# Half a tile of padding per expert in the steady list of pairs, the other pairs behind a branch

## The chip, the cores and the metric

The kernel runs on one core of one Trainium2 chip. The core has a matrix engine (TensorE, "PE" in the profile, with its weight loads as "PEld"), a vector engine (VectorE, "DVE"), an activation engine (ScalarE, "ACT"), GpSimd ("POOL") and SyncE ("SP"), which here issues most of the transfers. The metric is the device time of one execution in microseconds (us), lower is better. Times shown for a kernel are the median of its runs with the lowest and the highest beside it.

## The reference, cut to what matters

One transformer layer over `x` of shape (4, 2048, 256), 8192 tokens in all: an adaptive layer norm, causal attention with 16 heads of 16, a second adaptive layer norm, and a mixture of experts with one shared expert.

```
x = x + ga * attention(layernorm(x) * (1 + ca) + sa)
h = layernorm(x) * (1 + cb) + sb
x = x + gb * ffn(h)
```

In `ffn` each token is sent to 4 of 16 experts: sigmoid scores with a bias, the best 2 of 4 groups, then the best 4 experts in them. Expert e computes `silu(h @ w1[e].T) * (h @ w3[e].T)` with 192 inner columns, then `@ w2[e].T`, weighted by the token's normalised score. The shared expert does the same for every token without a weight. How many tokens an expert gets depends on the data.

## The kernel before, in words

**Blocks, phases, tiles, pairs.** Tokens are worked on in 16 blocks of 512. Two phases split the blocks: phase 0 is blocks 0 to 11 (6144 tokens), phase 1 blocks 12 to 15 (2048 tokens). Within a phase every token is written four times, once for each chosen expert, into an array `xs` sorted by expert, as a row of 272 numbers (the token, its four experts and weights, its place). Each expert's rows are cut into tiles of 256 rows (`TT`), and the last tile of an expert is padded. Two tiles, mostly of different experts, are a pair, the unit of the expert stage. Since the program is fixed and the counts are not, `Phase` (L102) provides for the worst padding, 255 rows for each of 16 experts: 56 pairs in phase 0 and 24 in phase 1, 80 in all.

**`find_tiles` (L491)** counts the tiles of each expert in a phase on VectorE, and writes a table with expert and first row of each tile. A tile past the last real one repeats the last one's place, is marked as nobody's, and its results go to rows that are never read. It is worked on in full like any other.

**Attention stage (to about 2810 us).** Per pair of heads, four kinds of work are woven by hand. Other work goes in as generators: a generator's `yield` names the point where it can stop, and `Background.pull(n)` (L76) advances it by n yields. In this stage yields also carry a price in VectorE and GpSimd time and are drawn from a budget. `send(n)` (L372) is one such generator: it loads block n after attention (L378), normalises it (`normalise`, L262, with one GpSimd instruction at L273), scales it on GpSimd (L392, four instructions), turns it on TensorE (L291), computes scores, ranks them (`route`, L297, with six GpSimd instructions at L338 and a VectorE sum at L342), counts places on TensorE (L426, `pk`), and scatters 4 x 4 groups of 128 rows to `xs` with 16 indirect transfers issued by GpSimd (L477). Blocks of phase 0 are sent in the attention stage.

**Expert stage (from about 2810 us).** The loop at L1482 goes over the 80 pairs m, three loads ahead. Per pair: SyncE reads four table entries into registers and issues two loads of weights (`wt`, 640 KB each, L1224) and two of rows (`xt`, 272 KB each, L1226). TensorE turns the rows (`turn`, L1240), makes the inner values (`gu`, L1255: 24 matmuls) in two parts, `inner_a` and `inner_b`, and the outer product (`y`, L1293 and L1304: 16 matmuls). ScalarE and VectorE do the sigmoids and products (`ha`, `hb`, L1266 to L1268). `give` (L1314) is called one pair late: VectorE works out weights and places (L1320 to L1347), ScalarE and VectorE move the products out of PSUM (`yt`, L1354, L1356), and GpSimd issues four indirect transfers that scatter them to `yd`, four rows a token (L1358). So the order on every engine is written out by hand, and an instruction that waits holds up all behind it on its engine.

**Background of the expert stage.** `other(2)`, `other(1)`, `other(2)` pull 5 yields a pair at three points: after `inner_a`, before `give`, after `inner_b`. In the 56 pairs of phase 0 the list is `late`: `send` of blocks 12 to 15 and `find_tiles` of phase 1, 62 yields a block and 9. It must be through three pairs before phase 1 begins (`late.drain`). From the second pair of phase 1 the list is `rest`, which is `back()`: for each of the 16 blocks, load (`fetch`, L1372, issued at L1375) the normalised block `hTs` and the block `base`, run the shared expert (`shared`, L1392 on: TensorE `sgu` at L1398 and `y` with `wsh`), and for the blocks of phase 0 `collect` (L1381, issued at L1386, one load of 2 MB, `yg<-yd`) and `combine` (L1438: sums of the four rows on VectorE and GpSimd, L1443 to L1449, and the store of `out`, L1450). A block of phase 0 takes 9 yields, one of phase 1 six, less one for the last. What is left of `rest` after the loop is drained there. Then the four blocks of phase 1 are collected and combined.

Of the kernel before, what the change touches and what calls it, by code (L numbers as in the profile page):

```python
# [8 lines left out]
F32 = mybir.dt.float32  # L9
# [3 lines left out]
I32 = mybir.dt.int32  # L13
AF = mybir.ActivationFunctionType
ALU = mybir.AluOpType
AX = mybir.AxisListType

P = 128
# [6 lines left out]
NB = B * NQ  # L25
E, I = 16, 192
EW = 2 * 2 * I + 2 * D
N = B * T
TT = 256
# [77 lines left out]
class Phase:  # L107


    def __init__(self, blocks):  # L110
        self.blocks = blocks
        self.tokens = len(blocks) * BT

        self.region = self.tokens + TT


        self.pairs = -(-((4 * self.tokens + E * (TT - 1)) // TT) // 2)


@with_exitstack  # L120
def adaln_attention_moe(
# [17 lines left out]
    nc = tc.nc  # L139
# [37 lines left out]
    phases = [Phase(blocks) for blocks in PHASES]  # L177
# [81 lines left out]

    between = const.tile([1, 1], F32, name="between")  # L260

    def normalise(xb, pools, xn):  # L262

        mv = pools.tile([P, 4, 2], F32, tag="mv", name="mv")
        for t in range(4):
            yield 0, 0.6, 0
            st = pools.tile([P, 6], F32, tag="bst", name="bst")
            nc.vector.bn_stats(st, xb[:, t, :])
            nc.vector.bn_aggr(mv[:, t, :], st)
        yield 0, 0.2, 1.0  # L270
        rs = pools.tile([P, 4], F32, tag="rs", name="rs")
        nc.vector.tensor_scalar_add(rs, mv[:, :, 1], EPS)
        nc.gpsimd.tensor_tensor(rs, rs, mhalf, ALU.pow)  # L273
        yield 0, 0, 0
        for t in range(4):
            if t % 2 == 0:
                yield 0, 0.9, 0
            nc.vector.tensor_scalar(
                xn[:, t, :], xb[:, t, :], mv[:, t, 0:1], rs[:, t : t + 1], ALU.subtract, ALU.mult
            )  # L280
        return xn
# [12 lines left out]
            evict(hT[:, k, :], pt, k)  # L294
        return hT

    def route(lg, tp):  # L297


        sc = tp.tile([P, 4, E], F32, tag="sc", name="sc")  # L300
        nc.scalar.activation(sc, lg, AF.Exp, scale=-1.0)
        yield 0, 0.6, 0
        nc.vector.tensor_scalar_add(sc, sc, 1.0)
        nc.vector.reciprocal(sc, sc)
        sb = tp.tile([P, 4, E], F32, tag="sb", name="sb")
        nc.vector.tensor_add(sb, sc, gbias.unsqueeze(1).to_broadcast([P, 4, E]))
        yield 0, 0.9, 0

        sg = sb.rearrange("p t (g e) -> p (t g) e", e=4)
        prs = tp.tile([P, 16, 6], F32, tag="prs", name="prs", bufs=1)  # L310
        nc.vector.tensor_add(prs[:, :, 0:3], sg[:, :, 0:3], sg[:, :, 1:4])
        nc.vector.tensor_add(prs[:, :, 3:5], sg[:, :, 0:2], sg[:, :, 2:4])
        nc.vector.tensor_add(prs[:, :, 5:6], sg[:, :, 0:1], sg[:, :, 3:4])
        gs = tp.tile([P, 4, 4], F32, tag="gs", name="gs")
        nc.vector.tensor_reduce(gs.rearrange("p t g -> p (t g)"), prs, AX.X, ALU.max)
        yield 0, 0.8, 0

        def ranks(v, k, allowed):

            full = [P, 4, k, k]  # L320
            other = v.unsqueeze(2).to_broadcast(full)
# [12 lines left out]
            for out, in0, in1, op in todo:  # L334
                for t in (slice(0, 2), slice(2, 4)) if k == E else (slice(0, 4),):
                    if k == E:
                        yield 0, 0, 1.1
                    eng.tensor_tensor(out[:, t], in0[:, t], in1[:, t], op)  # L338
            yield 0, 0, 0
            yield 0, 1.2 if k == E else 0.6, 0  # L340
            rk = tp.tile([P, 4, k], F32, tag=f"rk{k}", name=f"rk{k}")
            nc.vector.tensor_reduce(rk, gt, AX.X, ALU.add)  # L342
            return rk

        rg = yield from ranks(gs, 4, None)
        am = tp.tile([P, 4, E], BF, tag="am", name="am")
        nc.vector.tensor_scalar(
            am.rearrange("p t (g e) -> p (t g) e", e=4),
            rg.rearrange("p t g -> p (t g)").unsqueeze(2).to_broadcast([P, 16, 4]),
            2.0,  # L350
            None,
            ALU.is_lt,
        )
# [12 lines left out]
        nc.vector.tensor_mul(w, w, den.unsqueeze(2).to_broadcast([P, 4, E]))  # L366
        nc.vector.tensor_scalar_mul(w, w, 2.5)
        return re, ch, w

    modbs = [None, None]  # L370

    def send(n, xp, tp, psum, tag):  # L372

        ph = phase_of[n]
        yield 0, 0, 0
# [3 lines left out]
        if modbs[1] != n // NQ:  # L379
# [6 lines left out]
        for _ in range(3):  # L386
            yield 0, 0, 0
        h = yield from normalise(xb, tp, xb)
        for m, op in ((1, ALU.mult), (0, ALU.add)):
            for t in (slice(0, 2), slice(2, 4)):  # L390
                yield 0, 0, 1.3
                nc.gpsimd.tensor_tensor(  # L392
                    h[:, t], h[:, t], modbs[0][:, m, :].unsqueeze(1).to_broadcast([P, 2, D]), op
                )
        yield 0, 0, 0
        yield 1, 0, 0

        def evict(to, pt, k):
# [4 lines left out]
        yield 0, 0, 0  # L403
        yield 1, 0, 0
        lg = psum.tile([P, 4, E], F32, tag=tag, name="lg")
        for t in range(4):
            for k in range(2):
# [4 lines left out]
                    start=(k == 0),  # L412
                    stop=(k == 1),
                )
        re, ch, w = yield from route(lg, tp)
        yield 0, 0.2, 0
        chb = tp.tile([P, 4, E], BF, tag="chb", name="chb")
        nc.vector.tensor_copy(chb, ch)
        yield 0, 0, 0
        yield 1, 0.5, 0  # L420


# [64 lines left out]
                nc.gpsimd.memset(between, 0.0)  # L487

    tabs = ctx.enter_context(tc.tile_pool(name="tabs", bufs=1))

    def find_tiles(ph):  # L491

# [67 lines left out]
        nc.vector.tensor_scalar(real, which, last, None, ALU.is_le)  # L560
        nc.vector.scalar_tensor_tensor(tab[:, :, 2], tab[:, :, 0], 5.0, real, ALU.add, ALU.mult)
        nc.vector.tensor_scalar_add(tab[:, :, 2], tab[:, :, 2], -5.0)
        tabi = tabs.tile([P, 2, 3], I32, tag="tabi", name="tabi")
        nc.vector.tensor_copy(tabi, tab)
        tabd = dram.tile([pairs, 6], I32, name="tabd" + ph.name)
# [636 lines left out]
    def bank(name, shape=(P, 2 * TT)):  # L1202
        return banks.tile(list(shape), F32, tag="b", name=name)

    pairs = [(ph, i) for ph in phases for i in range(ph.pairs)]
    wts_, xts, xTs = {}, {}, {}
    issued = []

# [183 lines left out]
    def shared(n, hT):  # L1392
# [16 lines left out]
        ha = hp.tile([P, BT], F32, tag="sha", name="sha", bufs=1)  # L1409
        nc.scalar.activation(ha, g, AF.Sigmoid)  # L1410
        yield 0, 0, 0
        nc.vector.tensor_mul(ha, ha, g)
        nc.vector.tensor_mul(ha, ha, u)
        gu = up(2 * P)
# [2 lines left out]
        for half in range(2):  # L1417
# [2 lines left out]
            nc.scalar.activation(hb[rows, :], gu[:64, cols], AF.Sigmoid)  # L1420
            parts.append((hb[rows, :], gu[:64, cols], gu[64:, cols]))
        yield 0, 0, 0
        for to, g, u in parts:
            nc.vector.tensor_mul(to, to, g)
            nc.vector.tensor_mul(to, to, u)
        yield 0, 0, 0
        pss = outer(wsh.unsqueeze(1).to_broadcast([P, 2, EW]), ha, hb)
        yield 0, 0, 0
        y = hp.tile([P, 4, D], F32, tag="sy", name="sy", bufs=1)
        for half in range(2):  # L1430
# [39 lines left out]
    budget = Budget()  # L1470
    late, rest = Background(budget), Background(budget)
    for n in phases[1].blocks:
        late.add(send(n, lp, lp, banks, "b"))
    late.add(find_tiles(phases[1]))
    split, end = phases[0].pairs, len(pairs)

    for m in range(3):
        load(m)
    held = None
# [1 line left out]
    turn(0)  # L1481
    for m in range(end + 1):  # L1482

        def other(n):

            (late if m < split else rest).pull(n)

        if m == split + 1:
            rest.add(back())
        if m < end:  # L1490
            ha = inner_a(wts_[m], xTs[m])
            other(2)
# [12 lines left out]
        other(2)  # L1505
    rest.drain()
    for n in phases[1].blocks[:2]:
        collect(n)
    for n in phases[1].blocks:
        for _ in combine(n):  # L1510
            pass
        if n + 2 in phases[1].blocks:
            collect(n + 2)


def _rope():
# [69 lines left out]
```

## Time and profile before

| what | us |
|---|---|
| median of 3 runs | 3905.32 |
| lowest and highest of them | 3895.76, 3907.83 |
| the profiled execution's own time | 3907.39 |
| its span in the trace | 3905.7 |
| busy in the span: PE, PEld | 3298.8, 1723.2 |
| busy in the span: DVE, ACT, POOL | 2585.4, 1525.6, 1522.0 |

The span runs from the first to the last profiled instruction. A busy time is the union of the engine's instructions. A row `X <- Y` in a list of waits says that engine and line X waited for Y, with the total, how often, and the longest. The granted clock (PEclk) is the share of full speed at which TensorE was let run. `sgu`, `gu`, `yd` and the like are the program's names of tiles.

### The profile page before, as it was taken

What the parts mean: (1) busy time and instruction counts of PE and PEld (TensorE: products, weight loads), DVE (VectorE), ACT (ScalarE), POOL (GpSimd) and SP (SyncE); (2) the same over time, 40 slices, a digit from 0 to 9 for tenths busy, and PEclk for the clock granted to TensorE, in tenths of its full rate; (3) what the DMA queues carried; (4) which work ended last, traced back from release to release, by engine and by line L of the source; (5) the groups of instructions that cost most, each with busy time, mean ns of one, the idle gap of its engine ahead of it and who ended that gap; (6) DMA issues with size and microseconds to landing.
All of it is one profiled execution on the core that took longest, in us unless ns stands there. A gap on an engine that the chain in (4) does not pass through costs nothing. (4 is left out here: it accounts for less than half of the span.)

```text
span 3905.7 us, 56489 instructions
## 1 busy us (share of the span) xinstructions
PE 3298.8 (84%) x20276; PEld 1723.2 (44%) x20400; DVE 2585.4 (66%) x4650; ACT 1525.6 (39%) x2188; POOL 1522.0 (39%) x2216
## 2 busy tenths in 40 slices
PE   3677988979889889888888988899888888899994
PEld 1333433434334333333433333333477676676662
DVE  2365776767776767766676777677276576667775
ACT  0233544544455544444444544455422222222220
POOL 1321243333433353244335334210155555545554
PEclk6688988989899988988988998899999898899997
DMA  5423232331333232223323322220377666688763
GB/s 163 144 84 120 98 131 101 121 118 63 109 110 123 96 117 93 81 84 102 123 101 117 104 72 71 101 96 1 114 255 242 205 226 236 216 280 303 273 248 140
DMA packets 279212, 544.96 MB, mean 140 GB/s; under 512 B 27535, under 2 KB 151439, under 8 KB 278931
## 3 DMA queue, kind: packets, MB, share of 16 engines
q1 hardware_dynamic: 249106, 461.61, 34.8%
q0 software_dynamic: 27648, 77.63, 5.3%
q8 instruction: 161, 2.64, 0.3%
q10 hardware_dynamic: 2176, 2.10, 0.2%
q14 instruction: 121, 0.98, 0.1%
HBM read 351.42 MB, written 189.81 MB: 139 GB/s over the span
## 5 line engine op out<-in xcount | busy, mean ns | idle before, releaser
L888 DVE TENSOR_REDUCE mparts<-ps 128x2 f32<-128x1024 f32 (+3 forms) x1152 | 1180.5, 1044 | 465.1 <-PE ps L878 421.1
L1154 ACT ACTIVATE e<-st 128x1024 f32<-128x1024 f32 (+3 forms) x1280 | 1078.6, 895 | 1031.3 <-PE st L1146 954.8
L878 PE MATMUL ps<-kt,qt 64*128 64x512 f32 (+3 forms) x3328 | 616.2, 415 | 187.2 <-ACT e L1154 64.8
L1087 PE MATMUL po<-e,vg 128*32 128x512 f32 (+3 forms) x5120 | 667.8, 588 | 27.4 <-POOL e L1158 15.7
L878 PEld LDWEIGHTS ps<-kt,qt 64*128 64x128 f32 x3328 | 304.7, 204 | 778.2 <-ACT e L1154 437.9
L1158 POOL TENSOR_SCALAR_AFFINE_SELECT e<-e 128x256 f32<-128x256 f32 x512 | 204.6, 410 | 964.6 <-ACT e L1154 960.7
L1255 PE MATMUL gu<-xT,wt 128*128 128x256 f32 x1920 | 462.9, 396 | 20.4 <-issue 9.5
L1358 POOL DMA_INDIRECT yd<-yt,to x320 | 315.9, 987 | 393.0 <-ACT hb L1266 200.3
L1146 PE MATMUL st<-qt,kt 64*128 64x512 f32 (+3 forms) x2560 | 461.4, 441 | 0.0
L1255 PEld LDWEIGHTS gu<-xT,wt 128*128 128x128 f32 x1920 | 370.4, 197 | 108.6 <-issue 44.0
L1139 PE MATMUL st<-mt,pick 32*128 32x512 bf16 (+3 forms) x2560 | 302.7, 375 | 74.0 <-DVE mparts L888 46.9
L477 POOL DMA_INDIRECT xs<-row,rowx x256 | 248.4, 970 | 175.0 <-DVE row L468 120.3
L911 DVE TENSOR_REDUCE mparts<-ps 128x8 f32<-128x1024 f32 x128 | 156.7, 1224 | 202.4 <-PE ps L878 191.6
L1146 PEld LDWEIGHTS st<-qt,kt 64*128 64x128 f32 x2560 | 206.1, 199 | 139.2 <-issue 127.5
L1354 ACT ACTIVATE yt<-y,of 128x256 f32<-128x256 f32 x160 | 67.1, 470 | 400.0 <-DVE is L1334 200.6
L803 POOL TENSOR_TENSOR r<-qk,rp 128x512 f32<-128x512 f32 x120 | 154.4, 1305 | 168.4 <-DVE qk L780 164.8
L1139 PEld LDWEIGHTS <-pick 32*128 32x128 bf16 x2560 | 86.9, 92 | 297.3 <-issue 285.3
L1087 PEld LDWEIGHTS po<-e,vg 128*32 128x32 f32 x5120 | 109.2, 112 | 185.8 <-issue 126.5
L749 POOL TENSOR_TENSOR low<-whole,high 128x512 fp32r<-128x512 f32 x64 | 81.4, 1271 | 258.9 <-ACT whole L676 258.7
L1293 PE MATMUL y<-wt,ha 128*128 128x256 f32 x640 | 161.7, 391 | 21.6 <-issue 18.5
L1293 PEld LDWEIGHTS y<-wt,ha 128*128 128x128 f32 x640 | 119.3, 196 | 41.8 <-issue 24.1
L776 PE MATMUL pq<-wqkv,hT 128*128 128x512 f32 x240 | 128.3, 660 | 10.4 <-ACT whole L676 8.6
(218 smaller groups left out, 3603.2 us busy)
## 6 DMA issues: line engine op xcount, KB each, us to landing
wt<-in_w_all SPq DMA_DIRECT2D x160, 640.0 KB
kt<-kd SPq DMA_DIRECT2D x124, 512.0 KB
xt<-xs SPq DMA_DIRECT2D x160, 272.0 KB
qt<-qd SPq DMA_DIRECT2D x64, 512.0 KB
yg<-yd SPq DMA_DIRECT2D x16, 2048.0 KB
vg<-vd SPq DMA_DIRECT2D x124, 168.0 KB
xb<-in_x SPq DMA_DIRECT2D x32, 512.0 KB
qd<-high SPq DMA_DIRECT2D x128, 128.0 KB
```

What stands on the lines that cost most here:

```text
L477: s_ = nc.gpsimd.indirect_dma_start(out=ph.xs[:, :], out_offset=bass.IndirectOffsetOnAxis(ap=rowx[:, n, t, j : j + 1], axis=0), in_=row[:, ...
L878: nc.tensor.matmul(ps[:, half, to : to + width], lhsT=qt[rows, q, t * P : (t + 1) * P], rhs=kt[rows, q, key : key + width], start=start, s ...
L888: nc.vector.tensor_reduce(to, ps[:, :, :width], AX.X, ALU.max)
L911: nc.vector.tensor_reduce(mine[:, :, :, 0], ps.rearrange("p h (t k) -> p h t k", k=P), AX.X, ALU.max,)
L1087: nc.tensor.matmul(po[32 * j : 32 * j + 32, off:], lhsT=va[:, k_, j * (HD + 1) : j * (HD + 1) + 32], rhs=es[j // 2][:, j % 2, off:], start ...
L1139: nc.tensor.matmul(sts[q][:, h_, off:], lhsT=pick[rows, :], rhs=mt[rows, off:], start=True, stop=False,)
L1146: nc.tensor.matmul(sts[q][:, h_, off:], lhsT=kt[rows, q, k_ * P : (k_ + 1) * P], rhs=qt[rows, q, off:], start=False, stop=True,)
L1154: nc.scalar.activation(es[q][:, :, off:], sts[q][:, :, off:], AF.Exp, scale=SCALE)
L1158: nc.gpsimd.affine_select(out=es[q][:, :, off : off + P], in_=es[q][:, :, off : off + P], compare_op=ALU.is_ge, fill=0.0, base=0, pattern= ...
L1255: nc.tensor.matmul(ps[:, c_ * TT : (c_ + 1) * TT], lhsT=wt[:, c_, k * 2 * I + cols : k * 2 * I + cols + P], rhs=xT[:, k, c_ * TT : (c_ + 1 ...
L1293: nc.tensor.matmul(pss[half][:, t, :], lhsT=ha[:, at_ : at_ + P], rhs=wt[:, half, 4 * I : 4 * I + D], start=(t == 0), stop=False, skip_gro ...
L1358: s_ = nc.gpsimd.indirect_dma_start(out=ph.yd[:, :], out_offset=bass.IndirectOffsetOnAxis(ap=to[:, t : t + 1], axis=0), in_=yt[:, t, :], i ...
```

## The change

`Phase` gets a second number of pairs, `usual`, that provides for half a tile of padding an expert: 52 pairs in phase 0 and 20 in phase 1. The loop runs over these 72 pairs. The other 4 + 4 pairs, and a second making of all sums (shared expert, collecting, combining, for all 16 blocks), stand after the loop's end in a block that runs only if a number in memory, `beyond`, is over 0: `find_tiles` sets it to the tiles of a phase past `2 * usual`, the larger of the two phases. All engines read it into a register after the loop.

The background is spread otherwise. In the expert stage `late` is pulled 3, 2, 2 a pair and `rest` 5, 3, 4. `send` in this stage has `apart=3`: at the points where one engine's result is waited for, three empty yields in place of one (in the attention stage it stays at one). `shared` gets five more empty yields: one after each group of sigmoids, two before the outer product, and one after it. So a `send` has 76 yields in this stage, and a block of `rest` 14, or 11 in phase 1.

```diff
@@ class Phase
         self.pairs = -(-((4 * self.tokens + E * (TT - 1)) // TT) // 2)
+        self.usual = -(-(4 * self.tokens + E * TT // 2) // (2 * TT))
...
@@ normalise, route, send: empty yields
-        yield 0, 0, 0
+        for _ in range(apart):
+            yield 0, 0, 0
...
@@ find_tiles
+        many = small_tile("many", [P, 1])
+        nc.vector.tensor_scalar(many, last, float(1 - 2 * ph.usual), 0.0, ALU.add, ALU.max)
+        if ph is phases[0]:
+            nc.vector.tensor_copy(beyond, many)
+        else:
+            nc.vector.tensor_max(beyond, beyond, many)
+        nc.vector.tensor_copy(beyondi, beyond)
...
-    pairs = [(ph, i) for ph in phases for i in range(ph.pairs)]
+    pairs = [(ph, i) for ph in phases for i in range(ph.usual)]
+    split, end = phases[0].usual, len(pairs)
+    pairs += [(ph, i) for ph in phases for i in range(ph.usual, ph.pairs)]
...
@@ shared
         nc.scalar.activation(ha, g, AF.Sigmoid)
         yield 0, 0, 0
+        yield 0, 0, 0
...
         for to, g, u in parts:
             nc.vector.tensor_mul(to, to, g)
             nc.vector.tensor_mul(to, to, u)
+        for _ in range(3):
+            yield 0, 0, 0
+        pss = outer(wsh.unsqueeze(1).to_broadcast([P, 2, EW]), ha, hb)
         yield 0, 0, 0
-        pss = outer(wsh.unsqueeze(1).to_broadcast([P, 2, EW]), ha, hb)
         yield 0, 0, 0
...
     for n in phases[1].blocks:
-        late.add(send(n, lp, lp, banks, "b"))
+        late.add(send(n, lp, lp, banks, "b", 3))
...
-            (late if m < split else rest).pull(n)
+            if m < split:
+                late.pull((3, 2, 2)[k])
+            else:
+                rest.pull((5, 3, 4)[k])
...
     rest.drain()
+    more_tiles = nc.values_load(beyondi[0:1, 0:1], min_val=0, max_val=E)
     for n in phases[1].blocks[:2]:
         collect(n)
...
+    with tc.If(more_tiles > 0):
+        issued.clear()
+        for m in range(end, len(pairs)):
+            load(m)
+            turn(m)
+            ha = inner_a(wts_[m], xTs[m])
+            hb = inner_b(wts_[m], xTs.pop(m))
+            give(m, ha, hb)
+        for n in range(NB):
+            hT = fetch(n)
+            collect(n)
+            for gen in (shared(n, hT), combine(n)):
+                for _ in gen:
+                    pass
```

More of the change, by code (lines that the diff above doesn't have):

```diff
@@ L260, in adaln_attention_moe, with normalise @@
     between = const.tile([1, 1], F32, name="between")
-    def normalise(xb, pools, xn):
+    def normalise(xb, pools, xn, apart=1):
         mv = pools.tile([P, 4, 2], F32, tag="mv", name="mv")
@@ L295, in transposed, with route @@
         return hT
-    def route(lg, tp):
+    def route(lg, tp, apart):
         sc = tp.tile([P, 4, E], F32, tag="sc", name="sc")
@@ L338, in ranks @@
                     eng.tensor_tensor(out[:, t], in0[:, t], in1[:, t], op)
-            yield 0, 0, 0
+            for _ in range(apart):
+                yield 0, 0, 0
             yield 0, 1.2 if k == E else 0.6, 0
@@ L370, in adaln_attention_moe, with send, wait @@
     modbs = [None, None]
-    def send(n, xp, tp, psum, tag):
+    def send(n, xp, tp, psum, tag, apart=1):
+        def wait():
+            for _ in range(apart):
+                yield 0, 0, 0
         ph = phase_of[n]
@@ L385, in send @@
             modbs[0] = modb
-        for _ in range(3):
+        for _ in range(2 + apart):
             yield 0, 0, 0
-        h = yield from normalise(xb, tp, xb)
+        h = yield from normalise(xb, tp, xb, apart)
         for m, op in ((1, ALU.mult), (0, ALU.add)):
@@ L394, in send @@
                 )
-        yield 0, 0, 0
+        yield from wait()
         yield 1, 0, 0
@@ L402, in send @@
         nc.sync.dma_start(hTd[n], hT.rearrange("p k t -> p (k t)"))
-        yield 0, 0, 0
+        yield from wait()
         yield 1, 0, 0
@@ L414, in send @@
                 )
-        re, ch, w = yield from route(lg, tp)
+        re, ch, w = yield from route(lg, tp, apart)
         yield 0, 0.2, 0
@@ L418, in send @@
         nc.vector.tensor_copy(chb, ch)
-        yield 0, 0, 0
+        yield from wait()
         yield 1, 0.5, 0
@@ L489, in adaln_attention_moe @@
     tabs = ctx.enter_context(tc.tile_pool(name="tabs", bufs=1))
+    beyond = tabs.tile([P, 1], F32, name="beyond")
+    beyondi = tabs.tile([P, 1], I32, name="beyondi")
     def find_tiles(ph):
@@ L1411, in shared @@
         yield 0, 0, 0
+        yield 0, 0, 0
         nc.vector.tensor_mul(ha, ha, g)
@@ L1422, in shared @@
         yield 0, 0, 0
+        yield 0, 0, 0
         for to, g, u in parts:
@@ L1425, in shared @@
             nc.vector.tensor_mul(to, to, u)
+        for _ in range(3):
+            yield 0, 0, 0
+        pss = outer(wsh.unsqueeze(1).to_broadcast([P, 2, EW]), ha, hb)
         yield 0, 0, 0
-        pss = outer(wsh.unsqueeze(1).to_broadcast([P, 2, EW]), ha, hb)
         yield 0, 0, 0
@@ L1472, in adaln_attention_moe @@
     for n in phases[1].blocks:
-        late.add(send(n, lp, lp, banks, "b"))
+        late.add(send(n, lp, lp, banks, "b", 3))
     late.add(find_tiles(phases[1]))
-    split, end = phases[0].pairs, len(pairs)
     for m in range(3):
@@ L1482, in adaln_attention_moe, with other @@
     for m in range(end + 1):
-        def other(n):
-            (late if m < split else rest).pull(n)
+        def other(k):
+            if m < split:
+                late.pull((3, 2, 2)[k])
+            else:
+                rest.pull((5, 3, 4)[k])
         if m == split + 1:
@@ L1491, in adaln_attention_moe @@
             ha = inner_a(wts_[m], xTs[m])
-            other(2)
+            other(0)
             if m + 1 < end:
```

## The prediction, made before the changed kernel ran

> **What bounds the kernel now.** I read the page's slices first, then busy time by stretch, the waits, and the chain that ended last.
>
> ```profile
> PE   3677988979889889888888988899888888899994
> PEclk6688988989899988988988998899999898899997
> DMA  5423232331333232223323322220377666688763
> ```
>
> Each digit is a fortieth of the span (98 us). The change touches only what follows slice 29, the expert stage. TensorE is busy 8 or 9 tenths there and the transfers 6 to 8: TensorE is the likely bound, its clock and the transfers are to be watched.
>
> I cut the stage at starts of the first sigmoid (`ha`) of pairs 0, 51, 57 and 79, and took one stretch of four pairs (53 to 56) that have no background. Columns: stretch, length, busy time (instructions) of PE, PEld, DVE, ACT and POOL, granted clock, DMA share, GB/s.
>
> ```profile
> 2819.20:3418.70 599.50, 515.71 (x2556) 412.76 (x2556) 393.53 (x1122) 150.44 (x324) 326.20 (x566) 0.92 0.68 233
> 3435.40:3471.60 36.20, 36.20 (x194) 30.06 (x193) 23.74 (x73) 11.12 (x25) 17.13 (x33) 1.00 0.82 271
> 3471.60:3815.30 343.70, 317.07 (x1408) 228.78 (x1407) 252.76 (x528) 74.37 (x169) 182.60 (x209) 0.97 0.74 271
> 2948.00:2956.00 8.00, 3.34 (x16) 2.50 (x15) 1.68 (x4) 0.57 (x2) 6.67 (x14) 0.95 0.65 204
> 2956.00:2963.00 7.00, 2.13 (x5) 1.14 (x4) 0.00 (x0) 0.36 (x1) 3.13 (x6) 0.50 0.62 213
> ```
>
> A bare pair costs 36.20 / 4 = 9.05 us with TensorE busy throughout and DMA at 0.82, so transfers do not hold it up. The 51 pairs of the first row take 599.5 us; bare they would take 461.6. The background of four `send` thus costs 138 us. The last two rows show one part of that: while GpSimd issues indirect transfers without a pause, TensorE crawls, with "issue" (no wait that the profile shows) as the cause. Pairs 11, 22, 34 and 49, in each of which a block's scatter falls together with the pairs' own, take 22.5, 24.6, 21.6 and 20.8 us, together 53 over bare. The waits of 2819 to 3472 show a second part:
>
> ```profile
> PE pt L291 <- POOL row L392: 16.6, 7, 7.5
> PE pk L426 <- DVE ha L1267: 7.2, 1, 7.2
> PE pk L426 <- DVE chb L418: 4.6, 3, 2.0
> ```
>
> With 7.1, 3.6 and 2.9 us for `gu` and `y` on copies and `hb`, TensorE waits 42 us for a named engine. TensorE's own work for `send` is 18 us (7.5 `lg`, 7.2 `pt`, 3.8 `pk`). The remaining 25 are mostly low clock.
>
> **Part 1: eight pairs go.** Whether the branch is taken is decided by the data, not the profile. Routing the reference's inputs by its own formulas gives 103 tiles in phase 0 and 40 in phase 1, against limits of 104 and 40; the nearest expert is 21 tokens short of a further tile. So the block is skipped. The pairs that go from phase 0 are bare ones, since the background's amount stays: 4 x 9.05 = **36 us less**.
>
> **Part 2: `late` denser, with longer gaps.** Before, 4 x 62 + 9 = 257 yields at 5 a pair last to pair 51. After, 4 x 76 + 9 = 313 at 7 last to pair 44 of 52, before the drain at 49. Three yields of 7 are 3.9 us of a bare pair, one of 5 was 1.8. Of the 42 us of waits, the largest 7.5, I let a third stay: **28 less** (bounds: 0 and 42). Against it: 7 instead of 5 scatters fall between two pairs' own four. GpSimd issues one each 1.27 us (2938.50, 2939.76, 2941.03 in its timeline), so a pair takes it 11 x 1.27 = 14.0 us, against 9.05 on TensorE; before 11.4. The unbroken run of 2938.5 to 2959.8 was 21 us; the crawl began 11.5 us into it and ended about 3.5 after it, 13 in all. A run of two such pairs, 28 us, would give 28 - 11.5 + 3.5 = 20, 6.5 more a block: **26 more** (bounds: all 53 gone, if a shorter first run breaks it; 54 more, for a 35 us run over all 16 scatters and three pairs' own). I take 26, nearest to the rows. SP's `row` loads move up with their `send`; SP idles between issues, nothing waits longer. The added VectorE work of `find_tiles` (three instructions of 0.2 us at most, like L1342's 0.17) lies far ahead of its reader, in phase 0 under the attention of blocks 12 to 15.
>
> Phase 0: -36 - 28 + 26 = **-38**.
>
> **Part 3: phase 1.** From `ha` of its first pair to that of its last it took 9.05 (no background yet) + 343.7 = 352.8 us for 23 intervals. TensorE's shared work in the 343.7 is 113.4 us by the stretch of tile `wsh`; one block is 12 `sgu` in 5.3 and 16 `y` in 3.0, so 8.3 us, and 13.7 of 16 blocks fitted. 22 x 9.05 + 113.4 = 312.5, leaving 31.2 us of stall and low clock, 2.3 a block. After, 212 yields at 12 a pair end in the 18th pair with background, so all 16 blocks lie in the 19 intervals: 19 x 9.05 + 16 x 8.3 = 305. Stalls here are `y` of the shared expert waiting for its VectorE products:
>
> ```profile
> PE y L1293 <- DVE sha L1413: 12.8, 5, 3.5
> PE y L1304 <- DVE shb L1425: 4.8, 4, 2.2
> ```
>
> Formerly two steps that follow each other fell in one group of pulls, with nothing of the pairs between them, 2 times in 5 (groups 2, 1, 2). Three pulls apart in groups of 5, 3, 4 it is 3 in 12. Scaling 2.3 by 0.25 / 0.4 gives 1.4 x 16 = 23. So 305 + 23 = 328: **25 less** (bounds: 305, no stalls, 48 less; 343, the transfers as the limit, see the rivals, 10 less).
>
> **Part 4: the end.** From the last `ha` to the span's end it was 90.4 us. Here 14 yields of `rest` were left over:
>
> ```profile
> 3836.87 2.41 DMA yd<-yt,to
> 3839.77 8.73 DMA hTs<-hTd
> 3848.64 7.10 PE sgu L1398 x12
> 3860.50 4.42 DVE yg L1443 x2
> ```
>
> The chain goes through loading and computing the last shared block before the first final sum at 3860.5; from there 45.2 us to the end. After, nothing is left over: last `ha`, about 9 for the outer products and the last inner part, 1 for `yt`, 4 x 1.27 issues, 2.4 to land, 0.4 + 7.7 for the first `yg`, sums 45.2: 71 in all, **20 less**. A branch is added. All engines read `beyondi` (SP's pitch with a checked read is 1.11 us of which 0.35 is the issue, so 0.8 each, at once); on SP the read stands ahead of the last collects, which wait for `yd` anyway, on GpSimd behind the last scatters and ahead of sums that wait for VectorE. The jump itself is in no row of this trace. Bounds: 0.3 (two short SP instructions) and 12 (three closings like the last one, 3901.5 to 3905.7). I take **4**, one closing. So -16 (bounds -20 and -8).
>
> [...] This trace has the row of the fetches (queue, packets, MB, share of 16 engines), from straight-line code alone:
>
> ```profile
> q8 instruction: 161, 2.64, 0.3%
> ```
>
> [...]
>
> **Sum.** -38 - 25 - 16 = -79. The profiled execution's own time is 3907.4 (span 3905.7), 2.1 over the median of the runs. 3907.4 - 79 = **3828**.
>
> **Rivals.**
> *The crawl grows and eats phase 0* (12%). For it: POOL at 14.0 us a pair against 9.05. With a 35 us run, +54 instead of +26: 3856. At both bad bounds, no wait won back and the longest run, phase 0 gives 36 lost against 54, +18, and the sum 3885. Against it: a crawling TensorE delivers no results, and so breaks GpSimd's run.
> *Transfers limit phase 1* (8%). By bytes, bare pairs 36.20 x 271 / 4 = 2.45 MB; 343.7 x 271 less 22 of these leaves 2.9 MB a block; 19 and 16 of them are 93 MB, at the same 271 GB/s 343 us: 3843. Against it: at DMA 0.82 a bare pair has no wait, and these bytes need only 0.74 x 343.7 = 254 us of full DMA, 0.78 of 328.
> *The scatters break up and the crawl goes* (9%): 79 fewer for the 26 + 53: 3749.
> *Slower: the block runs* (4%), so the change doesn't do what it says. It decides at the 105th tile of phase 0 or the 41st of phase 1. Place: after the last sum. Price: 8 pairs without overlap, at least 9.05 and perhaps 15 with loads and sigmoids in line, and 16 blocks of at least 8.3 + 45.2 / 4 = 19.6: 72 + 314 to 120 + 314, so 4210 to 4260. Against it are the counts.
>
> **Numbers.** My forecast, 3828 with 3790 to 3860 as its own spread, has 67%, the four rivals 33%. For 8 in 10 the range reaches past the transfers and part way to both crawl cases: 3765 to 3875. About 0.3% (12 us) is what a measurement here can tell from no change. Faster by more than that: 0.93; within: 0.03; slower: 0.04.
>
> **What would show it.** Right: 144 loads of `wt`; bare pairs still 9.05; phase 1's 19 intervals near 328 us with all 16 shared blocks before the last pair; about 71 us from the last `ha` plus a few for the branch; POOL waits of `pt` and `pk` under 15 us. Wrong: a stretch over 25 us in phase 0 with TensorE under half busy; TensorE waiting for `wt` or `hTs` in phase 1; over 12 us between the last sum and the end.

## The result, and the profile after

| | before, us | after, us |
|---|---|---|
| median of 4 runs each | 3904.9 | 3856.49 |
| lowest and highest | 3895.76, 3907.83 | 3854.18, 3858.62 |
| the profiled execution's own time, and its span | 3907.39, 3905.7 | 3858.62, 3856.5 |

The ratio is 0.9877 (95% interval 0.986 to 0.9894): faster by 1.2%, 48.8 us in the profiled executions. The forecast was 79 us. The sign and the range hold; the size is 30 us short.

Cut at the same places as in the prediction, at starts of `ha`, the two spans differ so:

| stretch | before | after | difference | forecast |
|---|---|---|---|---|
| start to the first `ha` (attention, code unchanged) | 2819.2 | 2809.0 | -10.2 | 0 |
| phase 0: first `ha` to that of the first pair of phase 1 | 643.3 | 616.2 | -27.1 | -38 |
| phase 1: to the last `ha` | 352.8 | 360.4 | +7.6 | -25 |
| the end: last `ha` to the end of the span | 90.4 | 70.8 | -19.6 | -16 |

So phase 0 gave less than forecast, phase 1 became longer where it was to become shorter, and 10 us in the attention stage, which no step forecast, hide part of it: the three stages that the change touches give 39 us, half of the 79. The page's slices after (a slice is 96 us; the expert stage begins in the 30th):

```profile
PE   3776988979888988888898988899888798798893
PEclk7688989989999988988999998799988898899996
DMA  4423242331233322223333222211086666587763
```

The clock, the transfers and TensorE's busy share in the last ten slices are all a little lower than before, which speaks against the transfers as the limit: TensorE waits for something. The stretches show where (columns as in the prediction: stretch, length, busy time of PE, PEld, DVE, ACT, POOL, clock, DMA share, GB/s). They are phase 0 while `late` runs, seven bare pairs, phase 1, and the end.

```profile
2809.00:3371.00 562.00, 474.70 (x2310) 378.49 (x2310) 361.82 (x1037) 137.35 (x295) 307.45 (x527) 0.89 0.66 227
3371.00:3434.30 63.30, 63.30 (x338) 52.58 (x337) 41.33 (x127) 19.44 (x43) 29.98 (x59) 1.00 0.79 262
3434.30:3785.70 351.40, 313.30 (x1315) 216.04 (x1314) 251.65 (x489) 69.96 (x157) 178.51 (x182) 0.96 0.67 243
3785.70:3856.50 70.80, 9.51 (x47) 6.94 (x45) 24.77 (x42) 2.99 (x7) 31.15 (x30) 0.59 0.47 172
```

A bare pair is what it was, 63.30 / 7 = 9.04 us, with TensorE busy throughout. In the first row TensorE has 87 us without work, in the third 38. The waits of TensorE name who ended them (total, times, longest; all in us), for phase 0:

```profile
PE y L1316 <- issue: 26.1, 20, 2.2
PE pk L437 <- DVE chb L429: 9.9, 3, 5.2
PE gu L1278 <- DVE xT L1267: 9.4, 4, 5.1
PE pk L437 <- DVE ha L1290: 7.7, 1, 7.7
PE pt L295 <- POOL row L403: 7.5, 2, 5.2
```

and for phase 1:

```profile
PE y L1316 <- DVE sha L1437: 30.6, 9, 4.3
PE y L1327 <- DVE shb L1450: 7.1, 4, 3.8
```

In phase 0 `pt` has lost 9 us of its 16.6, but `pk` has grown from 11.8 to 17.6. With `gu`, 2.7 and 2.4 for `y` and 1.1 for `ptx`, about 41 us of named waits remain of 42. In phase 1 the wait for `sha` has grown from 12.8 us in 5 to 30.6 in 9.

What phase 0 gave adds up so. At 9.05 us each, 56 pairs are 506.8 us and 52 are 470.6: 36.2 less. TensorE's time without work in the phase went from 83.8 to 87.3 us (named waits 42.8 and 41.9 with the smallest rows, waits with no engine named 40.0 and 44.3). Its busy time over that of bare pairs, which is the work of `send` and low clock, went from 52.7 to 58.3. So -36.2 + 3.5 + 5.6 = -27.1.

Phase 1 holds more work than before. TensorE's matmuls with `wsh`, before and after (the columns are PE and PEld):

```profile
3471.60:3815.30 343.70, 113.40 (x344) 59.70 (x345) 0.97 0.74 271
3434.30:3785.70 351.40, 148.31 (x448) 78.18 (x448) 0.96 0.67 243
```

A block has 28 of them, so these are 12.3 blocks and 16. A block's own work is 8.3 us at full clock (the prediction's 5.3 + 3.0). Before, 22 x 9.05 + 12.3 x 8.3 = 301 of the 343.7 us are work, which leaves 43 us of stall and low clock, 3.5 a block. After, it is 360.4 - 305 = 55 us, 3.5 a block as well. So the phase has 3.7 blocks more at 11.8 us and four pairs less at 9.05, which makes it 7.5 us longer; 7.6 were measured.

The end is now a chain without a shared block in it. After the last four scatters:

```profile
3801.31 2.37 DMA yd<-yt,to
3803.69 7.84 DMA yg<-yd
3811.63 2.37 DVE yg L1470 x2
...
3847.71 2.32 POOL yg L1476
```

### The profile page after: what moved, and what is told of

It is laid out like the page before. It is cut to its first block, busy times and chain, and to the rows that moved or that the text cites. A ratio compares the mean times of both kernels' runs of the same rounds, so it can differ in the third digit from the quotient of the medians.

```text
span 3856.5 us, 55181 instructions
## 1 busy us (share of the span) xinstructions
PE 3226.3 (84%) x19892; PEld 1665.9 (43%) x20016; DVE 2535.0 (66%) x4512; ACT 1506.0 (39%) x2140; POOL 1491.4 (39%) x2152
## 5 line engine op out<-in xcount | busy, mean ns | idle before, releaser
L1278 PE MATMUL gu<-xT,wt 128*128 128x256 f32 x1728 | 416.5, 397 | 15.2 <-DVE xT L1267 9.4
L1381 POOL DMA_INDIRECT yd<-yt,to x288 | 283.0, 983 | 335.1 <-ACT yt L1377 142.7
L1278 PEld LDWEIGHTS gu<-xT,wt 128*128 128x128 f32 x1728 | 334.2, 198 | 93.8 <-issue 35.0
L1316 PE MATMUL y<-wt,ha 128*128 128x256 f32 x576 | 153.8, 407 | 29.1 <-issue 26.1
L1316 PEld LDWEIGHTS y<-wt,ha 128*128 128x128 f32 x576 | 111.4, 203 | 52.3 <-issue 36.5
```

Source lines behind the costliest of these rows:

```text
L1278: nc.tensor.matmul(ps[:, c_ * TT : (c_ + 1) * TT], lhsT=wt[:, c_, k * 2 * I + cols : k * 2 * I + cols + P], rhs=xT[:, k, c_ * TT : (c_ + 1 ...
L1316: nc.tensor.matmul(pss[half][:, t, :], lhsT=ha[:, at_ : at_ + P], rhs=wt[:, half, 4 * I : 4 * I + D], start=(t == 0), stop=False, skip_gro ...
L1381: s_ = nc.gpsimd.indirect_dma_start(out=ph.yd[:, :], out_offset=bass.IndirectOffsetOnAxis(ap=to[:, t : t + 1], axis=0), in_=yt[:, t, :], i ...
```

## Experiments

They ran on three chips, here A, B and C, whose times for the same kernel differ, so each is compared with kernels on its own chip. Stretches as above, in us, from each run's one profiled execution. "Stall" is the sum of TensorE's gaps of over 0.3 us in phase 1; in the profiles of the result it is 26.0 before and 37.2 after. The changed kernel itself did not run on chip A; the one without the branch stands for it there.

| run | median, ratio to before (95%) | phase 0 | phase 1 | stall | end |
|---|---|---|---|---|---|
| *chip A* (before: 3818.39) | | | | | |
| pairs only | 3769.64, 0.9886 (0.985 to 0.9922) | 560.9 | 287.3 | 21.0 | 134.5 |
| no branch | 3773.72, 0.9896 (0.9859 to 0.9934) | 565.2 | 357.0 | 36.3 | 68.2 |
| gap in the sums | 3785.79, 0.9916 (0.9886 to 0.9945) | 563.2 | 355.1 | 31.0 | 74.0 |
| two scatters a pair | 3754.0, 0.9843 (0.9804 to 0.9881) | 531.3 | 361.6 | 36.8 | 70.6 |
| *chip B* (before: 3829.4) | | | | | |
| before, again | 3815.72, one run | 589.0 | 352.6 | 26.1 | 90.4 |
| after, again | 3782.92, 0.9892 (0.9867 to 0.9917) | 562.7 | 360.2 | 35.7 | 70.9 |
| sums on VectorE | 3762.6, 0.9819 (0.9788 to 0.985) | 564.8 | 336.9 | 21.5 | 65.9 |
| both | 3725.28, 0.9739 (0.9715 to 0.9764) | 529.5 | 338.4 | 21.5 | 66.0 |
| *chip C* (before: 3892.93) | | | | | |
| after, a third time | 3851.32, 0.9883 (0.9858 to 0.9909) | 601.9 | 360.4 | 36.3 | 70.9 |
| apart 1 | 3913.35, 1.0037 (1.0011 to 1.0062) | 661.2 | 356.3 | 35.7 | 71.0 |
| old `rest` | 3864.62, 0.9931 (0.9905 to 0.9958) | 605.3 | 364.3 | 44.2 | 83.8 |
| both, even pulls | 3772.04, 0.9674 (0.9653 to 0.9695) | 555.6 | 337.6 | 21.6 | 65.9 |

The attention stage ran from 2770 to 2820 us in these kernels with the same code, with a spread of 22 to 26 us among the kernels of one chip. The 10.2 us of the result's first row can't be told from that.

### The same two kernels on other chips

> The kernel before once more, unchanged, for its stages on the same chip as the next three. Both theories: phase 1 about 353 us and the end about 90 from the last ha; phase 0 between the 643 of the first trace and the 597 that the kernel with old background and 52 pairs implies (561 + 4 x 9.05); if the crawl without a named wait belongs to the chip and not to the program, it is missing wherever the whole time is near 3818.

> The changed kernel once more, unchanged, as the reference for the next two on the same chip. Phase 1 about 360 us and the end about 71 on any chip; phase 0 about 565 us without the crawl, 616 with it.

> The changed kernel once more, unchanged, as the reference on the same chip as the next three. Phase 1 about 360 us and the end about 71; phase 0 about 563 us without the crawl, 616 with it.

On chip B the differences after less before are -26.3, +7.6 and -19.5 us: those of the result within a microsecond, so they belong to the kernels. But phase 0 itself is 54 us shorter there in both, and the crawl is absent. The next two fences are stretches of the changed kernel while GpSimd issues its transfers almost without a pause. In the profile of the result, inside pair 9:

```profile
2917.00:2930.00 13.00, 3.00 (x6) 1.72 (x6) 1.68 (x4) 0.75 (x2) 10.82 (x21) 0.53 0.44 167
```

On chip B, two stretches inside pairs 10 to 12:

```profile
2875.50:2893.50 18.00, 18.00 (x97) 14.96 (x96) 11.84 (x36) 5.50 (x12) 14.95 (x29) 1.00 0.82 297
2893.50:2915.50 22.00, 11.70 (x53) 9.27 (x52) 8.19 (x27) 2.67 (x7) 13.11 (x25) 0.74 0.63 228
```

In the first fence, six matmuls get through in 13 us. On chip B TensorE works at full clock through 18 us of the same, and then stops once: 10.3 us for `xT` (L1267). That copy was late because VectorE stood before it, at the first instruction of the next block's `send`. The waits of VectorE and of SyncE's queue on chip B, after:

```profile
DVE bst L271 <- DMA row<-x1d: 36.1, 3, 12.7
SPq L389 <- DMA xs<-row,rowx: 55.8, 10, 15.5
```

and before:

```profile
DVE bst L268 <- DMA row<-x1d: 23.0, 3, 9.4
SPq L378 <- DMA xs<-row,rowx: 42.9, 6, 14.5
```

`row` has one buffer. The load of the next block (L389) stands on SyncE until the last of the 16 scatters that read the old one has landed, and then VectorE, which comes to it a few yields later, waits for the load. At 7 yields a pair it comes there sooner: 36.1 us in place of 23.0. Pairs 12, 22 and 33 take 22.0, 19.8 and 19.3 us, 34 over bare; in 22 and 33 TensorE waits 7.8 and 7.3 us for `xt`, whose loads stand behind that of `row` in SyncE's queue. In sum, TensorE's time without work in phase 0 on chip B went from 50.0 to 59.6 us, all of it with a named engine, and its busy time over bare pairs from 32.2 to 32.5: -36.2 + 9.6 + 0.3 = -26.3. So nearly the same gain comes about in another way than in the result. Chip C has the crawl again (pairs of 24.1, 17.1, 19.6, 18.5, 19.9 and 17.4 us, 62 over bare) and 1.9 us of waits for `row`.

### The pairs alone

```diff
-        late.add(send(n, lp, lp, banks, "b", 3))
+        late.add(send(n, lp, lp, banks, "b"))
-                late.pull((3, 2, 2)[k])
+                late.pull((2, 1, 2)[k])
-                rest.pull((5, 3, 4)[k])
+                rest.pull((2, 1, 2)[k])
```

and `shared` without its five new empty yields.

> The 72 pairs and the branch stay; the background goes back to what it was (pulls 2, 1, 2 for both lists, apart 1, no added yields in shared). Theory: the new spacing gained nothing in phase 0 (its longer runs of indirect transfers ate what it saved) and is needed in phase 1 only to get the shared blocks done in the loop. So phase 0 (first ha of pair 0 to that of pair 52) about 607 us against 616 in the changed kernel, phase 1 to the last ha about 300 against 360, but 34 yields (4 to 5 shared blocks) left after the loop, so about 165 from the last ha to the end against 71: in all about 3885. Rival, the forecast's view that longer gaps save 28 us of waits in phase 0: phase 0 about 640 and in all about 3915.

Phase 0 is far from the rival's 640 us. That it is also under the theory's 607 says little: 607 was reckoned with the crawl, and chip A, like B, has no wait of TensorE without a named engine in phase 0. TensorE makes only 280 matmuls with `wsh` in phase 1, so 10 shared blocks, and 6 are left for the end. The expert stage takes 560.9 + 287.3 + 134.5 = 982.7 us with its branch, against 990.4 for the change without a branch (the next run) on the same chip. The medians are the same within their intervals. Where there is no crawl, the new order of the background gives nothing in sum: the time comes from the shorter list. Eight bare pairs are 72 us; the shared blocks that they covered come back as 44 us at the end (134.5 against 90.4), or as stalls in phase 1 when they are squeezed in.

### No branch

`values_load` and the block behind it are left out.

> The changed kernel without the register read and without the block behind the branch (right for these inputs, since the block does not run). Theory: the branch costs 2 to 4 us, the part of the 3.7 us jump on SP that the landing of the last store does not cover: about 3853. Rival: the 10 us by which the expert stage began earlier in the changed kernel's trace come from the program's new layout and go with the block: the expert stage begins near 2819 us and the whole is about 3863.

The end is 68.2 us, against 70.6 to 71.0 in five profiles with the branch and the same sums: the register read and the branch together cost 2.6 us. In the trace of the changed kernel SyncE's compare-and-branch is at 3850.48 and its next instruction at 3854.21, 3.7 us, partly beside the landing of the last store. VectorE has 2.9 between the two; GpSimd has 2.6, but in 2.3 of these its last sum still runs. Queue q14, which the page lists with the kind "instruction", moves six packets of 8 KB in the last 10 us of the changed kernel, from 3847.4 on, 1 us after VectorE's branch, and none in the last 31 us of the kernel without the branch, nor in the last 97 us of the kernel before. In the whole execution they don't show: 160 packets on q8 and 123 on q14 in the changed kernel against 161 and 121 before.

The rival falls, since the expert stage begins at 2780.8 us here, among the 2770.0 to 2791.6 of the kernels with the block on chip A.

### Where the stalls of phase 1 come from

**Another place in the group.** Two more empty yields in `combine` between GpSimd's sum (L1471) and VectorE's product (L1473), with `rest` at 5, 4, 4.

> In combine two empty yields are added between GpSimd's first sum and the VectorE product that waits for it, and rest is pulled 5, 4, 4 so that it still ends in the loop. Theory: VectorE stands still for that sum because both fall in one group of pulls, the shared expert's products queue behind it, and TensorE waits for them (37 us of waits and 31 us at half clock in phase 1); with the gap under 20 us of waits, phase 1 about 335 us instead of 360, in all about 3831. Rival: 0.84 blocks a pair are simply more than VectorE can do in time: waits stay over 30 us, in all within 6 us of 3856.

Phase 1 is 355.1 us against 357.0, TensorE's gaps are 31.0 us where under 20 was expected, and VectorE still waits 19.7 us for that sum (23.8 in the change, by the lists of its waits). The theory that these two steps in one group of pulls are the cause falls. In all the kernel is 12 us slower than the one without the branch.

**Sums on VectorE.** GpSimd's three sums of `shared` and `combine` are made by VectorE:

```diff
-        nc.gpsimd.tensor_tensor(bases[n], bases[n], y, ALU.add)
+        nc.vector.tensor_add(bases[n], bases[n], y)
...
-        nc.gpsimd.tensor_tensor(yg[:, :, 0], yg[:, :, 0], yg[:, :, 1], ALU.add)
+        nc.vector.tensor_add(yg[:, :, 0], yg[:, :, 0], yg[:, :, 1])
...
-        nc.gpsimd.tensor_tensor(yg[:, :, 0], yg[:, :, 0], base, ALU.add)
+        nc.vector.tensor_add(yg[:, :, 0], yg[:, :, 0], base)
```

> The three sums of a block that GpSimd makes in shared and combine go to VectorE, nothing else changes. Theory: while GpSimd makes a sum of 2.35 us VectorE's next instruction stands still (0.17 us ones take 2.3), and VectorE waits for the sum as well, so VectorE loses some 7 us a block and gives 3 x 1.2 in return; the shared products are then in time: TensorE's waits in phase 1 under 15 us instead of 37, phase 1 about 325 us instead of 360, the end about 58 instead of 71, in all about 45 us less than the changed kernel. Rival: VectorE has too much work per pair whoever holds it up, and 59 us more make it worse: phase 1 at least 355 us.

Phase 1 falls by 23.3 us to 336.9, two thirds of what was expected, and the end by 5.0, less than half; TensorE's gaps fall to 21.5 and not under 15. By the medians it is 20 us less than the changed kernel, not 45. The rival, that VectorE has too much to do, falls, since VectorE does more now. The two stretches of phase 1 on chip B, with the sums on VectorE:

```profile
3364.60:3701.50 336.90, 314.51 (x1361) 218.95 (x1361) 269.07 (x547) 72.77 (x163) 82.01 (x151) 0.98 0.74 261
```

and after, as it is:

```profile
3336.60:3696.80 360.20, 324.24 (x1363) 225.66 (x1362) 257.74 (x506) 72.85 (x162) 182.66 (x190) 0.94 0.68 243
```

A part of the reason is in these rows of the changed kernel's timeline (start, duration, engine, instruction):

```profile
3528.37 2.35 POOL L1471 TENSOR_TENSOR yg<-yg 128x1024 f32<-128x1024 f32 x1 [1.16 <-DVE here L1343]
3528.41 2.34 DVE L1357 TENSOR_TENSOR is<-here,xt 128x16 f32<-128x16 f32 x1
3530.87 0.17 DVE L1357 TENSOR_TENSOR is<-here,sml 128x16 f32<-128x16 f32 x1
```

A VectorE instruction that takes 0.17 us took 2.34, as long as the GpSimd sum beside it. By groups (count, busy, mean ns), all over phase 1 of the changed kernel:

```profile
L1470 DVE TENSOR_TENSOR yg<-yg 128x1024 f32<-128x1024 f32 x24 | 46.7, 1979 | 0.0
L1357 DVE TENSOR_TENSOR is<-here,xt 128x16 f32<-128x16 f32 x19 | 18.5, 972 | 0.6
```

and with the sums on VectorE:

```profile
L1470 DVE TENSOR_TENSOR yg<-yg 128x1024 f32<-128x1024 f32 x24 | 28.5, 1222 | 0.0
L1357 DVE TENSOR_TENSOR is<-here,xt 128x16 f32<-128x16 f32 x19 | 3.3, 175 | 0.6
```

33 us of VectorE's busy time in these two lines alone went with GpSimd's sums (the first two rows are the result's; on chip B they are 46.8 and 18.5); in the rows shown VectorE's short instruction lasts as long as the sum beside it, 2.34 us beside 2.35. What holds it up, no row shows. The other part is that VectorE no longer waits for GpSimd's result: the 23.8 us of waits for L1471 are gone too. Against both stand 49 us of new sums on VectorE (19.6, 14.7 and 14.7 in its lines). No run takes away one of the two parts alone.

**Old `rest`.** `shared` without the five new yields and `rest` at 3, 2, 2; the rest is the change.

> The changed kernel with shared as before (no added yields) and rest pulled 3, 2, 2, so that as many blocks are done per pair. Theory: phase 1's waits come from VectorE standing behind GpSimd's sums, and the added yields put the consumer later and save some of it: TensorE's waits in phase 1 rise from 37 to about 55 us, phase 1 from 360 to about 380. Rival: the added yields gain nothing, phase 1 within 6 us of 360.

Phase 1 is 364.3 us against 360.4, by this number the rival's side. But it holds one block less (420 matmuls with `wsh` against 448), TensorE's gaps grow from 36.3 to 44.2, and the block that is left makes the end 13 us longer. So at this density the added yields with their pulls are worth 17 us in the two stages, 13 by the medians; less than the theory had, more than the rival.

### What the empty yields of `send` are worth

The pulls stay at 3, 2, 2, and `send` goes back to one empty yield a point:

```diff
-        late.add(send(n, lp, lp, banks, "b", 3))
+        late.add(send(n, lp, lp, banks, "b"))
```

> The changed kernel with apart 1 in the late blocks, so without their 56 added empty yields; pulls stay 3, 2, 2. Theory: what TensorE waits for in phase 0 is set by how densely GpSimd's work is issued, and 7 pulls a pair undo the longer gaps; without them phase 0 is longer by 20 to 40 us than the changed kernel's (the waits for pt, pk and ha return in full and come denser). Rival: the empty yields save nothing, phase 0 within 8 us of the changed kernel's.

Phase 0 grows by 59 us to 661.2, far above what was expected, and the kernel is 0.4% slower than before. The waits of TensorE in its phase 0:

```profile
PE pt L295 <- POOL row L403: 32.5, 7, 9.2
PE pk L437 <- DVE chb L429: 24.5, 3, 10.5
PE y L1316 <- issue: 21.3, 23, 1.7
PE gu L1278 <- issue: 11.6, 12, 2.3
PE pk L437 <- DVE ha L1290: 10.4, 1, 10.4
```

So the gaps do what they are for: `pt` and `pk` wait 67 us without them and 23 with them (5.8, 9.9 and 7.7 on chip C). What the forecast left out is the other side: seven pulls a pair first made these waits longer than five did, at which they are 27 to 29 us in three profiles (before in the result and on B, the pairs alone on A).

### Two scatters a pair

The scatters of `send` get a list of their own, pulled 1, 0, 1, `late` is pulled 2, 2, 2, and `row` gets a second buffer, since with one the next load stands until the last scatter has landed (55.8 us on chip B):

```diff
+    rows_out = Background(Budget())
...
-        row = xp.tile([P, 4, ROW], F32, tag="xs", name="row")
+        row = xp.tile([P, 4, ROW], F32, tag="xs", name="row", bufs=2 if apart > 1 else 1)
...
-                late.pull((3, 2, 2)[k])
+                late.pull((2, 2, 2)[k])
+                rows_out.pull((1, 0, 1)[k])
```

> The 16 scatters of a late block stand in a list of their own and go out at 2 a pair beside the rest of late (2, 2, 2 a pair), with a second buffer for the block's rows; nothing is left out. Theory: TensorE's crawl (about 80 us over four blocks) comes from unbroken runs of indirect transfers of more than 11 us; with 6 a pair there is none, no pair over 20 us in phase 0, phase 0 about 540 us instead of 616, in all about 3776. Rival: the crawl belongs to the scatter of a block at any pace (its amount, or its targets): four or more pairs over 18 us stay, in all within 15 us of 3856.

Together with the sums on VectorE:

> The scatters at 2 a pair in a list of their own and the three sums on VectorE, both at once. Theory: the gains lie in different stages and add: 30 to 80 us less in phase 0 (by chip) and 45 less in phase 1 and the end, in all 75 to 125 us less than the changed kernel. Rival: VectorE's added sums also come into what phase 0 leaves, or TensorE then meets the transfers in phase 1: no more than 50 us less.

and on the chip with the crawl, with `rest` at 4, 4, 4:

> The best so far (scatters at 2 a pair in a list of their own, the three sums on VectorE) with rest pulled 4, 4, 4 in place of 5, 3, 4. Theory of the forecast: a wait arises where two steps fall in one group of pulls; three yields apart fall in one group 3 times in 12 in either split, so phase 1 stays within 5 us of its 338. Rival: the group of 5 is what puts VectorE's burst ahead of the shared products; phase 1 under 328.

Phase 0 is 33.9 us shorter on chip A (531.3 against 565.2) and 35.3 on chip B (529.5 against 564.8), with no pair over 15 us; no wait of VectorE for `row` is left. These chips had no crawl to lose. On chip C phase 0 is 46.3 shorter (555.6 against 601.9) and the largest pair takes 17.5 us, so the rival, a crawl at any pace, falls. The crawl is small there, but not quite gone: TensorE's waits with no engine named are 10.6 us in place of 38.9, and GpSimd still has unbroken runs of up to 15 us, which the theory had ruled out. The two gains add: by the medians 58 us less than the change on chip B, under the 75 expected and over the rival's 50, and 79 on chip C. The last kernel has the lowest ratio to before, 0.9674 (0.9653 to 0.9695). Its groups of 4, 4, 4 change nothing in phase 1, 337.6 against 338.4, as its theory had it.

These kernels changed the spacing and the buffer together. On chips A and B the 36 us of waits for `row` that vanished are the size of the gain, so the buffer is the likelier part there; on chip C that wait was 1.9 us, so there the spacing is the likelier part. No run has one without the other.

## Why the prediction was right and wrong, point by point

- **The block is skipped: right.** The page has `wt` loaded 144 times, for 72 pairs.
- **Eight pairs at a bare pair's price: right in the price**, 9.04 us. The 36 us of phase 0 weren't seen whole: with the pairs alone it is 560.9 us on A against 589.0 on B, both without crawl, 28 less. The other 8 lie in pair 49, which takes 18.7 us with the pairs alone and 9.05 before: the drain three pairs ahead of phase 1 comes before a list of 5 a pair has run out, and its last yields fall into that one pair. In the changed kernel the list is through by pair 44.
- **Phase 0, "I let a third stay: 28 less": wrong.** 41 of 42 us of named waits stay. The step took the waits of 5 pulls a pair and set longer gaps against them; at 7 pulls without the longer gaps the named waits were 81 us (67 of them for `pt` and `pk`). The gaps took back what the density cost, and little more. Outside the pairs of the crawl phase 0 did get 20 us shorter over bare (83 to 64), but named waits are only 5 of these; the rest wasn't followed.
- **Phase 0, "SP idles between issues, nothing waits longer": wrong.** In the profiles of the result SyncE's wait at the load of `row` grew from 1.0 to 20.0 us. Chip B shows it without a crawl over it: SyncE stands 55.8 us at the load of `row` in place of 42.9, and VectorE 36.1 in place of 23.0. The single buffer of `row` was in the code, and the first profile had only 2.2 us for it.
- **Phase 0, the crawl, "26 more": the number is right, in part by luck.** Six pairs (9, 20, 21, 31, 32, 42) take 30.0, 17.2, 21.3, 18.9, 20.5 and 28.5 us, 82 over bare; the forecast was 53 + 26 = 79. The mechanism, one run of GpSimd's transfers of 28 us, held for the first block (27.6 us) and about for the last (25.1); those of the other two blocks went in two runs of 16 to 19 us each. And 8 of the 82 us are named waits; those with no engine named grew by only 4 us in the phase, from 40.0 to 44.3. On chip B phase 0 became 26 us shorter with no crawl at all.
- **Phase 1, "13.7 of 16 blocks fitted" and "scaling 2.3 by 0.25 / 0.4": wrong, and the largest miss.** The 305 us of work stand, and all 16 blocks lie in the loop as forecast; but stall and low clock are 360.4 - 305 = 55 us, not 23: 37 of gaps, and most of the rest goes with a granted clock of 0.96. Two steps failed. The first took 113.4 us of busy time for full-speed work and divided it by a block's 8.3. By count, 344 matmuls of 28 a block, 12.3 blocks fitted, 102 us of work, and the stall was 3.5 us a block, not 2.3. The second scaled it down by how often two steps fall in one group of pulls. It stayed at 3.5. Unscaled, 16 x 3.5 = 56 us, the sum would have been 361. The groups count for less than the step had it: more room in one moved phase 1 by 2 us, and the old yields, with which such steps fall in one group 4 times in 7 and not 3 in 12, left 364.3 - 19 x 9.05 - 15 x 8.3 = 68 us, 4.5 a block, where the scaling would have more than doubled it. The even groups tell nothing here, since by the same rule they were to change nothing. Sums taken off GpSimd moved phase 1 by 23 us, to 2.0 a block. What the rest comes from is open.
- **The end, 71 + 4: right in its steps, with the branch at 2.6** instead of 4 and a chain of 68.2 instead of 71. The bounds of 0.3 and 12 hold it. The jump itself, 3.7 us from SyncE's branch to its next instruction with packets on q14 at that time, lies partly beside the landing of the last store.
- **The start: not forecast.** -10.2 us in code that is the same; other kernels spread as far. It is luck that it brings the total nearer to the forecast.
- **The rivals.** Transfers did not limit phase 1: it moved 360.4 x 243 = 87.6 MB, not 93, DMA is at 0.67, and TensorE waits for VectorE. The crawl did grow, as in the first rival's mechanism, but by the amount of the main forecast; that the median comes out at that rival's 3856 is chance, since phase 1 supplied the missing time. The crawl did not go, and the block did not run.

## What to carry to other kernels

When a list of background work is packed into fewer steps, price each engine's queue again at the new density: the waits in the old profile are those of the old density (here 27 to 29 us for `pt` and `pk` at 5 pulls a pair, 67 at 7 without the longer gaps). Count how many pieces of work a stage held by their instructions, not by busy time divided by the price of one: here 113 us of busy time held 102 us of work. Look for buffers with one copy whose next load stands behind the stores that read it (on chip B SyncE stood 55.8 us at the load of `row`), and for short VectorE instructions that last as long as the GpSimd sum beside them (2.34 us in place of 0.17); here three such sums a block moved to VectorE made VectorE busier, 269.1 us of phase 1 against 257.7 on chip B, and the stage 23 us shorter. Count what was hidden behind padding before you take its full price: with the pairs alone 72 us of bare pairs went and 44 us of shared blocks came back at the end.

## What the runs showed of the chip

- **A crawl in some of the runs.** In the profiles of the result and on chip C, after some 11 to 13 us of unbroken indirect transfers by GpSimd, TensorE crawls with no engine named: in the result it took only six matmuls in 13 us, at a granted clock of 0.53. It isn't TensorE alone: about the same time two issues of SyncE took 0.72 and 0.70 us in place of 0.33, and ScalarE and VectorE show gaps of 12.2 and 11.6 us put down to "remote" and "issue". On chips A and B runs of up to 45 us had none of it: TensorE's waits with no engine named in phase 0 are 0 there, 40.0 and 44.3 us in the result, 38.9 on C. With at most two scatters of `send` in a pair 10.6 were left on C. What it is stays open, and so does whether it belongs to the chip.
- **A jump over a block of code** took 3.7 us on SyncE from the branch to its next instruction, beside packets on q14, of the kind "instruction", and with the register read 2.6 us of the time.
- **The same kernel from chip to chip**: the medians of before are 3818.39, 3829.4 and 3892.93 us on A, B and C and 3904.9 in the result. Between the profiles of before on B and of the result 54 of the 92 us lie in phase 0 and 37 in the attention stage. The ratios of the change, 0.9877, 0.9892 (B) and 0.9883 (C), agree nevertheless.
